# Attention and routed experts in one kernel: three routing groups, row clearing by AND, zero fills after the attention, a different pacing at the end, and two chunks of angles on GpSimd

## The chip, the cores and the metric

The kernel runs on one core of one Trainium2 chip. A core has a matrix engine (TensorE, PE in the profile; PEld is its weight load), VectorE (DVE), ScalarE (ACT), GpSimd (POOL) and SyncE (SP, which here only issues DMAs). Each engine works through its own list of instructions in order; semaphores tie the lists together, and 16 DMA engines move data. The metric is the device time of one launch in microseconds (us), as the median of several runs.

## The reference

Input is x of shape 16 x 512 x 128 (16 sequences of 512 tokens), all in float32. Two blocks follow each other.

```python
# block 1: causal linear attention, 16 heads of 8
q, k, v = split(silu(x @ Wq)), split(silu(x @ Wk)), split(x @ Wv)
q, k = lrpe(q, theta), lrpe(k, theta)     # concat(t * cos(theta * n), t * sin(theta * n)), n the position
energy = einsum('bhnd,bhmd->bhnm', q, k) * tril
out = merge(einsum('bhnm,bhmd->bhnd', energy, v)) @ Wo * sigmoid(x @ G1 @ G2)
x = layernorm(x + layernorm(out) * gamma + beta)
# block 2: 8 experts, each token goes to its two best, 1280 places per expert
probs = softmax(rmsnorm(x) @ router_w.T);  topk_p, topk_i = top_k(probs, 2)
# expert e takes the first 1280 of its tokens in order; places past its count weigh 0
eout = (silu(xg @ rg) * (xg @ ru)) @ rd
routed = zeros.at[dispatch].add(eout * weight)
shared = silu(x @ sg) * (x @ su) @ sd
x = layernorm(x + shared + routed)
```

There are T = 8192 tokens in 64 tiles of 128 (NT), four tiles or chunks to a sequence (NC).

## The kernel before

**The stages.** First come the loads and small constants, then the attention with the routing, then the experts, then the end, in which the routed rows are added and normed. The shared branch (`shared_steps`) is a filler of matmul work that runs beside the other stages. It is a list `feed` of 384 steps: for each sequence 16 "up" steps (gate at L134, up at L147; two for each of eight slices of 128) and 8 "down" steps (L157), the down steps of a sequence standing behind the first four up steps of the next. The order of PE, ScalarE, VectorE and GpSimd is written out by the program (`manual_schedule`).

**The opening.** The attention needs cosine and sine of theta times position for the four chunks of a sequence. `angles(c, th)` makes the reduced angle on VectorE, `sines(c)` the values on ScalarE, `same(c)` a copy of half of them. Chunks 0 and 1 are made ahead of the first step; chunks 2 and 3 at the loop's steps t=0 and t=1 (`beginning`). The causal mask and a block mask are made by GpSimd. Two tiles of constants are filled by ScalarE (`nought`): `zero` at t=0 and `empty` at t=1. From t=1 to t=16 `fill` issues one DMA a step on SP's queue: eight of 1 MB that zero `y_dram`, and eight of 660 KB that write `empty` (a row of zeros with the target number NOBODY) to `xg_dram`.

**The attention loop** runs t from -2 to 64, one chunk of 128 tokens a step. A step projects chunk t+2 (`project`: queries, keys, values and gate, then the multiply `hat`, L448), transposes chunk t+1 (`turn_over`), makes the energies of chunk t (L506 on PE, the masked copies `et` at L513 on VectorE), and the values of chunk t-1 (L530 to L548), and keeps a running state (`remember`; its addition L495 is on GpSimd). Up to two shared steps lie in a step once a sequence is ready, from t=14 on. When a sequence has ended, `after(b)` (turns over some ten steps) projects the output, norms twice and makes the router's logits. It has an addition on GpSimd, L564.

**Routing.** The list `groups` says which sequences are routed together: seven groups. `route(b0, b1)` is a generator of some 30 small VectorE instructions over [128, tiles, 8] with one Exp on ScalarE and two matmuls for the prefix sums. `sprinkle` puts up to seven of its steps into an attention step and three into a step behind it. A routed tile gives two scatters: indirect DMAs by GpSimd that send its 128 rows of 132 numbers (x, token number, expert, two weights) to places in `xg_dram` (L733). They go two a step in the attention, one in two steps behind it.

**Behind the attention** (called the tail here) a second loop goes on with one shared step each until turns, routes and scatters are done, and 12 steps more (`over`).

**The experts.** `load_expert` brings weights and 1280 rows; `turn_rows` transposes rows by PE (L899) and copies them (L900) in three parts of 512, 512 and 256 rows; `targets_of` takes target row and weight out of the extra columns (L907 to L913). For each part four slices of gate and up (L1008, L1010), the product (L1013), and `back`, which multiplies by rd (L922), weighs (L926) and scatters to `y_dram` (L928). The next expert's rows are turned in the slots `aside` of the part before, one slot a slice. A row whose target is out of bounds is not written.

**The end** runs what is left of `feed`. `add_up` adds the two routed rows of a sequence, on every other step; `finish_lot` takes a lot (four tiles of a sequence, or one tile in the last sequence) through statistics of each tile, the root, the scaled copies (L981) and the store. `an_end` calls the first of three open lots that can go on; it is called once a step, and the loop goes on when `feed` is empty.

Of the kernel before, what the change touches and what calls it, by code (L numbers as in the profile page):

```python
# [10 lines left out]
F32 = mybir.dt.float32  # L11
# [8 lines left out]
P = 128  # L20
# [8 lines left out]
NOBODY = 1.0e6  # L29
# [17 lines left out]
def tile_kernel(  # L47
# [46 lines left out]
    idx = keep.tile([P, 2, NT], I32, name="idx")  # L94
    sg_sb = keep.tile([P, IS], F32, name="sg_sb")
# [95 lines left out]
    groups = [(0, 4), (4, 8), (8, 10), (10, 12), (12, 14), (14, 15), (15, 16)]  # L191
    with ExitStack() as ph:
# [21 lines left out]
        with tc.manual_schedule(engines=ORDERED):  # L214
# [63 lines left out]
            def nought(tile_, n):  # L278
                nc.scalar.copy(tile_, zcol.to_broadcast([P, n]))
# [3 lines left out]
            th_sb = cst.tile([P, D + HALF], F32, name="th_sb")  # L283
# [14 lines left out]
            zero = hp.tile([P, 4 * N], F32, tag="h", name="zero")  # L298
            empty = hp.tile([P, NS, R], F32, tag="h", name="empty")
            scratch = hp.tile([P, 10, D + HALF], F32, tag="h", name="scratch")  # L300
            turns_of = cst.tile([P, D + HALF], F32, name="turns_of")
# [32 lines left out]
        with tc.manual_schedule(engines=ORDERED):  # L334
# [27 lines left out]
            count = cst.tile([P, E], F32, name="count")  # L362
# [4 lines left out]
            toki = cst.tile([P, NT], I32, name="toki")  # L367

        def constants_of_routing():
# [12 lines left out]
            nc.vector.tensor_copy(x1[:, :, D], toki)  # L382

        def beginning(t):

            if t == -1:
                sines(1)
            elif t == 0:
                angles(2, th_sb)
                sines(2)  # L390
            elif t == 1:
                angles(3, th_sb)
# [12 lines left out]


        y_rows = y_dram.rearrange("(p q r) d -> p q (r d)", p=P, r=4 * N // D)
        x_rows = xg_dram.rearrange("(p q r) d -> p q (r d)", p=P, r=NS)

        def fill(i):  # L410
            if i < 8:
                nc.sync.dma_start(y_rows[:, i, :], zero)
            elif i < 16:
                nc.sync.dma_start(x_rows[:, i - 8, :], empty.rearrange("p r d -> p (r d)"))

        hats, qkt, ets, states, gates, oTs = {}, {}, {}, {}, {}, {}
# [211 lines left out]
        def route(b0, b1):  # L628
# [75 lines left out]
            inside = wide("inside")  # L704
# [9 lines left out]
            rank = wide("rank")  # L714
# [83 lines left out]
        with tc.manual_schedule(engines=ORDERED):  # L798
            for t in range(-2, NT + 1):
# [14 lines left out]
                if 1 <= t < 17:  # L814
                    fill(t - 1)
# [31 lines left out]
            while turns or todo or scatters or over:  # L847
                if not (turns or todo or scatters):
                    over -= 1
# [11 lines left out]
                if t % 2 == 0:  # L861
                    scatter_behind(latest[0])
                t += 1


    with ExitStack() as ph:
# [23 lines left out]
        xgTs, targets = {}, {}  # L890
# [11 lines left out]
        def targets_of(e):  # L902
# [6 lines left out]
            nc.vector.scalar_tensor_tensor(to, second, float(T), xg[:, :, D], ALU.mult, ALU.add)  # L909
            wt = ep.tile([P, NS], F32, tag="wt", name=f"wt_{e}")  # L910
# [81 lines left out]
        with tc.manual_schedule(engines=ORDERED):  # L992
            load_expert(0)
            load_expert(1)
            for o0, n in parts:
                turn_rows(0, o0, n)
            targets_of(0)
            backs = []
            for e in range(E):
                rg_sb, ru_sb, rd_sb, _ = got[e]  # L1000
                for o0, n in parts:
                    aside = []
                    if o0 == parts[1][0] and e + 1 < E:
                        aside = [lambda q=q: turn_rows(e + 1, *q) for q in parts] + [lambda: targets_of(e + 1)]
# [29 lines left out]
            while feed or ends:  # L1034
# [16 lines left out]
                an_end()  # L1051

# [44 lines left out]
```

## Time and profile before

| | |
|---|---|
| median of three runs | 878.83 us (878.65 to 879.22) |
| the profiled execution | 876.59 us, its span 874.7 us |
| mean granted PE clock | 0.987 |
| PE busy | 826.3 us, 94% |
| VectorE busy | 554.1 us, 63% |
| ScalarE busy | 449.4 us, 51% |
| GpSimd busy | 334.2 us, 38% |
| L412, fill of `y_dram` | 8 DMAs of 1024 KB, 11.5 us to landing |
| L414, fill of `xg_dram` | 8 DMAs of 660 KB, 9.2 us to landing |
| L733, scatters to `xg_dram` | 128, 1039 ns each, from 181.6 to 494.6 us |
| L928, scatters to `y_dram` | 80, 972 ns each, from 516.8 to 726.5 us |

The span is cut into 40 slices of 21.9 us in some rows: each digit is the busy share of a slice in tenths, and PEclk the TensorE clock that was granted, in tenths of the full one. A line of the timeline has start and duration in us, engine, source line, operation, the tile written and those read, and the number of instructions merged; in brackets stands the idle time ahead of it and what ended it. A line of the waits has who waited and for whom, the sum in us, how often, and the longest.

### The profile page before, as it was taken

To read this page: it belongs to the slowest core of one execution; us is meant where nothing else is said; L and a number is where in the kernel's file an instruction comes from. 1 tells how busy PE (TensorE), PEld (TensorE's weight loads), DVE (VectorE), ACT (ScalarE), POOL (GpSimd) and SP (SyncE) were. 2 spreads that over 40 slices of the span, in tenths; PEclk is the share of its full clock that TensorE was granted. 3 is DMA by queue.
4 is the path that set the end of the run, shared out by engine and by line. 5 is a ranking of instruction groups with operands and counts; after the bars stand their busy time and mean duration, and the time that the engine had idled before them with its cause. 6 is when DMAs were issued, how large, how long until landed. Compare 5 with 4: busy or idle time off the path is not lost. (4 is left out here: it accounts for less than half of the span.)

```text
span 874.7 us, 24501 instructions
## 1 busy us (share of the span) xinstructions
PE 826.3 (94%) x9792; PEld 567.3 (65%) x9792; DVE 554.1 (63%) x1705; ACT 449.4 (51%) x1302; POOL 334.2 (38%) x443
## 2 busy tenths in 40 slices
PE   6789999999989999999999999999999999999993
PEld 4566667667855765766666657777676776666663
DVE  7588888998888888978533343333333324785454
ACT  7677777577776767564322223333333332433434
POOL 2122222156655556486766413433333431001100
PEclk9899999999999999999999999999999999999997
DMA  7881111011111110000000233322132003650011
GB/s 215 323 343 34 32 34 33 30 36 58 58 40 52 57 52 27 22 29 16 11 6 1 87 88 92 95 80 65 60 92 64 25 25 112 178 169 25 25 37 48
DMA packets 64340, 62.87 MB, mean 72 GB/s; under 512 B 6180, under 2 KB 55132, under 8 KB 63202
## 3 DMA queue, kind: packets, MB, share of 16 engines
q1 hardware_dynamic: 57426, 50.35, 18.4%
q0 software_dynamic: 6656, 10.69, 3.7%
q8 instruction: 77, 1.26, 0.6%
q10 hardware_dynamic: 144, 0.26, 0.1%
q14 instruction: 37, 0.30, 0.1%
HBM read 32.62 MB, written 31.88 MB: 74 GB/s over the span
## 5 line engine op out<-in xcount | busy, mean ns | idle before, releaser
L733 POOL DMA_INDIRECT xg_dram<-x,idx x128 | 133.0, 1039 | 42.1 <-issue 36.7
L136 ACT ACTIVATE sl<-pg 128x512 f32<-128x512 f32 x128 | 76.2, 596 | 125.4 <-PE pg L134 124.6
L1013 DVE TENSOR_TENSOR eh<-esl,peu 128x512 f32<-128x512 f32 (+1 forms) x96 | 57.5, 599 | 127.8 <-PE peu L1010 127.8
L928 POOL DMA_INDIRECT y_dram<-y,to x80 | 77.8, 972 | 154.1 <-ACT y L926 154.1
L148 DVE TENSOR_TENSOR h<-sl,pu 128x512 f32<-128x512 f32 x128 | 87.5, 684 | 77.0 <-PE pu L147 64.6
L134 PE MATMUL pg<-x1T,sg_sb 128*128 128x512 f32 x256 | 131.9, 597 | 1.5 <-ACT sl L136 0.7
L147 PE MATMUL pu<-x1T,su_sb 128*128 128x512 f32 x256 | 131.0, 593 | 1.0 <-ACT sl L136 1.0
L513 DVE TENSOR_TENSOR et<-pe,causal 128x384 f32<-128x384 f32 x256 | 124.4, 547 | 9.6 <-PE pe L506 9.5
L157 PEld LDWEIGHTS pd<-sd_sb,h 128*128 128x128 f32 x1024 | 118.7, 192 | 5.8 <-issue 5.2
L157 PE MATMUL pd<-sd_sb,h 128*128 128x128 f32 x1024 | 121.9, 275 | 0.2 <-DVE add L494 0.2
L110 POOL TENSOR_TENSOR rstd<-ve,neghalf 128x4 f32<-128x4 f32 x44 | 47.2, 1073 | 194.2 <-DVE ve L108 168.0
L922 PEld LDWEIGHTS ped<-rd,eh 128*128 128x128 f32 x640 | 84.0, 192 | 24.6 <-issue 22.7
L1008 PE MATMUL peg<-xgT,rg 128*128 128x512 f32 (+1 forms) x192 | 84.6, 522 | 0.0
L1010 PE MATMUL peu<-xgT,ru 128*128 128x512 f32 (+1 forms) x192 | 84.4, 521 | 0.0
L922 PE MATMUL ped<-rd,eh 128*128 128x128 f32 x640 | 84.3, 275 | 0.0
L1012 ACT ACTIVATE esl<-peg 128x512 f32<-128x512 f32 (+1 forms) x96 | 50.5, 526 | 55.9 <-PE peg L1008 53.9
L147 PEld LDWEIGHTS pu<-x1T,su_sb 128*128 128x128 f32 x256 | 45.7, 190 | 46.0 <-issue 39.9
L926 ACT ACTIVATE y<-ped,wt 128x128 f32<-128x128 f32 x80 | 29.4, 368 | 84.6 <-PE ped L922 84.6
L134 PEld LDWEIGHTS pg<-x1T,sg_sb 128*128 128x128 f32 x256 | 44.3, 191 | 38.4 <-issue 33.7
L506 PE MATMUL pe<-q,kT 32*64 32x192 f32 x2048 | 62.1, 341 | 3.3 <-issue 2.8
L423 PE MATMUL pq<-W,xT 128*128 128x384 f32 x128 | 60.3, 554 | 4.6 <-ACT vlow L444 2.6
L448 DVE TENSOR_TENSOR hat<-qk,cst_tok 128x512 f32<-128x512 f32 x64 | 45.0, 704 | 20.4 <-ACT qk L431 20.3
(178 smaller groups left out, 1260.4 us busy)
## 6 DMA issues: line engine op xcount, KB each, us to landing
y_dram<-zero SPq DMA_DIRECT2D x8, 1024.0 KB, 11.5
y<-y_dram SPq DMA_DIRECT2D x32, 256.0 KB, 3.3
xT<-xt SPq DMA_DIRECT2D x15, 384.0 KB, 3.1
xg_dram<-empty SPq DMA_DIRECT2D x8, 660.0 KB, 9.2
xg<-xg_dram SPq DMA_DIRECT2D x8, 660.0 KB, 4.5
x<-x SPq DMA_DIRECT2D x16, 256.0 KB, 3.5
o<-res SPq DMA_DIRECT2D x15, 256.0 KB, 2.3
xg_dram<-x,idx POOLq DMA_INDIRECT x128, 2.3
```

What stands on the lines that cost most here:

```text
L134: nc.tensor.matmul(pg, sg_sb[:, ts(i, P)], seq, start=True, stop=True)
L136: nc.scalar.activation(sl, pg, AF.Silu)
L147: nc.tensor.matmul(pu, su_sb[:, ts(i, P)], seq, start=True, stop=True)
L148: nc.vector.tensor_tensor(h[i // half][:, i % half, :], h.pop(("s", i)), pu, ALU.mult)
L157: nc.tensor.matmul(pd, h[k][:, i - k * half, ts(c, P)], sd_sb[:, i, :], start=(i == 0), stop=(i == IS // P - 1))
L506: nc.tensor.matmul(pes[g][mine, s], kT[rows, s, mine], q2[rows, s, 3 * i : 3 * i + 3], start=(s == 0), stop=(s == 1),)
L513: nc.vector.tensor_tensor(et.rearrange("p s k n -> p s (k n)"), pes[g].rearrange("p s k n -> p s (k n)"), causal.rearrange("p k n -> p (k ...
L733: i = nc.gpsimd.indirect_dma_start(out=xg_dram[:, :], out_offset=bass.IndirectOffsetOnAxis(ap=idx[:, k, t : t + 1], axis=0), in_=x1[:, t, ...
L922: nc.tensor.matmul(pd, h[:, i, ts(c, P)], got[e][2][:, i, :], start=(i == 0), stop=(i == IR // P - 1))
L928: i = nc.gpsimd.indirect_dma_start(out=y_dram[:, :], out_offset=bass.IndirectOffsetOnAxis(ap=to[:, at : at + 1], axis=0), in_=y, in_offset ...
L1008: nc.tensor.matmul(pg[:, :n], rg_sb[:, ts(i, P)], xgTs[e][:, ds(o0, n)], start=True, stop=True)
L1010: nc.tensor.matmul(pu[:, :n], ru_sb[:, ts(i, P)], xgTs[e][:, ds(o0, n)], start=True, stop=True)
```

## The change

The routing groups become three: sequences 0 to 5, 6 to 11 and 12 to 15. `inside` and `rank` use the buffers of `sel` and `prob`.

`empty` and its eight fills of `xg_dram` are dropped, so places that no token takes hold whatever memory held. `clear_rows` sets such rows to zero after the load by an AND with a mask made from the expert's `count`, and their targets are put out of bounds by an OR. It is called part by part ahead of `turn_rows`, for expert 0 ahead of all of them, for the others in the slots `aside`, which now run over from the second part into the third.

The fills of `y_dram` become 16 of 512 KB, read from 512 zero columns in the first `vpads` tile, and are issued in the tail, one in four steps. The tail goes on until they are issued.

In the end `an_end` is called a second time on every odd step, and on every step when `feed` is empty.

The angles of chunks 2 and 3 (the third and fourth) are made by GpSimd, right behind its masks, in nine instructions each; at t=0 and t=1 VectorE makes only the absolute value, now by an AND that clears the sign bit.

```diff
-    groups = [(0, 4), (4, 8), (8, 10), (10, 12), (12, 14), (14, 15), (15, 16)]
+    groups = [(0, 6), (6, 12), (12, 16)]
...
+        def sizes(c):
+            nc.vector.tensor_scalar(
+                scratch[:, NC + c].bitcast(I32), scratch[:, c].bitcast(I32), 0x7FFFFFFF, None, ALU.bitwise_and
+            )
+
         def angles(c, th):
-            a, size, k, whole = scratch[:, c], scratch[:, NC + c], scratch[:, 8], scratch[:, 9]
+            a, size, by = scratch[:, c], scratch[:, NC + c], scratch[:, 2 * NC]
             both = ((slice(0, D), pos[:, 0, c : c + 1]), (slice(D, D + HALF), pos[:, 1, c : c + 1]))
+            on_vector = c < 2
+            engine = nc.vector if on_vector else nc.gpsimd
             for m, at in both:
-                nc.vector.tensor_scalar(k[:, m], turns_of[:, m], at, MAGIC, ALU.mult, ALU.add)
-            nc.vector.tensor_scalar(whole, k, MAGIC, -C1, ALU.subtract, ALU.mult)
+                engine.tensor_scalar(size[:, m], turns_of[:, m], at, MAGIC, ALU.mult, ALU.add)
+            engine.tensor_scalar(a, size, MAGIC, -C1, ALU.subtract, ALU.mult)
             for m, at in both:
-                nc.vector.scalar_tensor_tensor(a[:, m], th[:, m], at, whole[:, m], ALU.mult, ALU.add)
-            nc.vector.tensor_scalar(k, k, MAGIC, -C2, ALU.subtract, ALU.mult)
-            nc.vector.tensor_tensor(a, a, k, ALU.add)
-            nc.vector.scalar_tensor_tensor(size, a, -1.0, a, ALU.mult, ALU.max)
-            nc.vector.tensor_scalar(a, a, -PI_BELOW, PI_BELOW, ALU.max, ALU.min)
+                if on_vector:
+                    engine.scalar_tensor_tensor(a[:, m], th[:, m], at, a[:, m], ALU.mult, ALU.add)
+                else:
+                    engine.tensor_scalar(by[:, m], th[:, m], at, None, ALU.mult)
+            if not on_vector:
+                engine.tensor_tensor(a, a, by, ALU.add)
+            engine.tensor_scalar(size, size, MAGIC, -C2, ALU.subtract, ALU.mult)
+            engine.tensor_tensor(a, a, size, ALU.add)
+            if on_vector:
+                sizes(c)
+            engine.tensor_scalar(a, a, -PI_BELOW, PI_BELOW, ALU.max, ALU.min)
...
+            for c in range(2, NC):
+                angles(c, th_sb)
...
         def beginning_done(t):
-            if t == 0:
-                nought(zero, 4 * N)
-            elif t == 1:
-                nought(empty.rearrange("p r d -> p (r d)"), NS * R)
-                nc.gpsimd.memset(empty[:, :, D], NOBODY)
-            elif t == 2:
+            if t == 2:
                 constants_of_routing()
...
-                if 1 <= t < 17:
-                    fill(t - 1)
...
+            zero = vpads[0][0].rearrange("p a b d -> p (a b d)")[:, 0:N]
+            nought(zero, N)
-            while turns or todo or scatters or over:
-                if not (turns or todo or scatters):
+            while turns or todo or scatters or fills or over:
+                if not (turns or todo or scatters or fills):
                     over -= 1
...
+                if t % 4 == 1 and fills:
+                    fill(fills.pop(0))
...
+        def clear_rows(e, o0, n):
+            if o0 == 0:
+                taken[e] = ok = ep.tile([P, 2, NS], I32, tag="ok", name=f"ok_{e}")
+                nc.vector.tensor_scalar(ok[:, 0], slotno, count[:, e : e + 1], -1.0, ALU.is_lt, ALU.mult)
+                nc.vector.tensor_scalar(ok[:, 1], slotno, count[:, e : e + 1], float(NOBODY), ALU.is_ge, ALU.mult)
+            here = slice(o0 // P, (o0 + n) // P)
+            rows = got[e][3][:, here, :].bitcast(I32)
+            nc.vector.tensor_tensor(
+                rows, rows, taken[e][:, 0, here].unsqueeze(2).to_broadcast([P, n // P, R]), ALU.bitwise_and
+            )
...
+            nc.vector.tensor_tensor(to, to, taken[e][:, 1], ALU.bitwise_or)
...
+            for o0, n in parts:
+                clear_rows(0, o0, n)
             for o0, n in parts:
                 turn_rows(0, o0, n)
...
-                        aside = [lambda q=q: turn_rows(e + 1, *q) for q in parts] + [lambda: targets_of(e + 1)]
+                        for step in (clear_rows, turn_rows):
+                            aside += [lambda q=q, f=step, e=e: f(e + 1, *q) for q in parts]
+                        aside.append(lambda e=e: targets_of(e + 1))
...
                 an_end()
+                if begun % 2 == 1 or not feed:
+                    an_end()
```

More of the change, by code (lines that the diff above doesn't have):

```diff
@@ L28 @@
 R = D + 4
-NOBODY = 1.0e6
+NOBODY = 1 << 20
 LN_EPS = 1e-5
@@ L94, in tile_kernel @@
     idx = keep.tile([P, 2, NT], I32, name="idx")
+    count = keep.tile([P, E], F32, name="count")
+    slotno = keep.tile([P, NS], F32, name="slotno")
     sg_sb = keep.tile([P, IS], F32, name="sg_sb")
@@ L282, in tile_kernel @@
             nc.tensor.matmul(pth, ones[0:1, :], th_row, start=True, stop=True)
-            th_sb = cst.tile([P, D + HALF], F32, name="th_sb")
+            th_sb = wk1.tile([P, D + HALF], F32, tag="w", name="th_sb")
             nc.scalar.copy(th_sb, pth)
@@ L297, in tile_kernel @@
             cst_tok = cst.tile([P, NC, 2, 16, 2, 8], F32, name="cst_tok")
[L298 to L301, printed above, removed]
+            scratch = hp.tile([P, 2 * NC + 1, D + HALF], F32, tag="h", name="scratch")
+            turns_of = wk1.tile([P, D + HALF], F32, tag="o", name="turns_of")
@@ L361, in tile_kernel @@
             startrow = cst.tile([P, E], F32, name="startrow")
-            count = cst.tile([P, E], F32, name="count")
             goes_on = {}
@@ L367, in tile_kernel @@
             toki = cst.tile([P, NT], I32, name="toki")
+            sloti = cst.tile([P, NS], I32, name="sloti")
         def constants_of_routing():
@@ L382, in constants_of_routing @@
             nc.vector.tensor_copy(x1[:, :, D], toki)
+            nc.gpsimd.iota(sloti, pattern=[[P, NS]], base=0, channel_multiplier=1)
+            nc.vector.tensor_copy(slotno, sloti)
         def beginning(t):
@@ L388, in beginning @@
             elif t == 0:
-                angles(2, th_sb)
+                sizes(2)
                 sines(2)
             elif t == 1:
-                angles(3, th_sb)
+                sizes(3)
                 sines(3)
         def beginning_done(t):
-            if t == 0:
-                nought(zero, 4 * N)
-            elif t == 1:
-                nought(empty.rearrange("p r d -> p (r d)"), NS * R)
-                nc.gpsimd.memset(empty[:, :, D], NOBODY)
-            elif t == 2:
+            if t == 2:
                 constants_of_routing()
-        y_rows = y_dram.rearrange("(p q r) d -> p q (r d)", p=P, r=4 * N // D)
-        x_rows = xg_dram.rearrange("(p q r) d -> p q (r d)", p=P, r=NS)
+        y_rows = y_dram.rearrange("(p q r s) d -> q p r (s d)", p=P, r=2, s=N // D)
         def fill(i):
[L411 to L414, printed above, removed]
+            nc.sync.dma_start(y_rows[i], zero.unsqueeze(1).to_broadcast([P, 2, N]))
+        fills = list(range(2 * T * D // (P * 2 * N)))
         hats, qkt, ets, states, gates, oTs = {}, {}, {}, {}, {}, {}
@@ L703, in route @@
             nc.scalar.copy(tots[:, :, 1:], pin[:, 1].rearrange("p t e -> p e t"))
-            inside = wide("inside")
+            inside = rp.tile([P, n, E], F32, tag="sel", name=f"inside_{b0}")
             nc.scalar.copy(inside, pin[:, 0])
@@ L713, in route @@
             yield
-            rank = wide("rank")
+            rank = rp.tile([P, n, E], F32, tag="prob", name=f"rank_{b0}")
             nc.vector.tensor_tensor(rank, sums[:, :, :n].rearrange("p e t -> p t e"), inside, ALU.add)
@@ L888, in load_expert @@
             got[e] = rg_sb, ru_sb, rd_sb, xg
-        xgTs, targets = {}, {}
+        xgTs, targets, taken = {}, {}, {}
+        def clear_rows(e, o0, n):
[8 more added lines that the diff above has]
+            )
         def turn_rows(e, o0, n):
@@ L995, in tile_kernel @@
             for o0, n in parts:
+                clear_rows(0, o0, n)
+            for o0, n in parts:
                 turn_rows(0, o0, n)
             targets_of(0)
-            backs = []
+            backs, aside = [], []
             for e in range(E):
@@ L1001, in tile_kernel @@
                 for o0, n in parts:
-                    aside = []
                     if o0 == parts[1][0] and e + 1 < E:
-                        aside = [lambda q=q: turn_rows(e + 1, *q) for q in parts] + [lambda: targets_of(e + 1)]
+                        for step in (clear_rows, turn_rows):
+                            aside += [lambda q=q, f=step, e=e: f(e + 1, *q) for q in parts]
+                        aside.append(lambda e=e: targets_of(e + 1))
                     h = ep.tile([P, IR // P, N], F32, tag="eh", name=f"eh_{e}_{o0}")
```

## The prediction

> **What bounds the kernel now.** I read the page's slices first, then TensorE's waits in the opening, then the starts of the 64 hat multiplies (L448, one per attention step), and last the stretch behind the last matmul.
>
> ```profile
> PE   6789999999989999999999999999999999999993
> PEclk9899999999999999999999999999999999999997
> DMA  7881111011111110000000233322132003650011
> GB/s 215 323 343 34 32 34 33 30 36 58 58 40 52 57 52 27 22 29 16 11 6 1 87 88 92 95 80 65 60 92 64 25 25 112 178 169 25 25 37 48
> ...
> q8 instruction: 77, 1.26, 0.6%
> ```
>
> TensorE (PE) sets the time: busy 826.3 of 874.7 us. The 48.4 us of idle lie at both ends: 16.3 us before 60 us (windows 0:20, 20:40, 40:60), where the DMA engines are full, and 13.9 us behind the last shared matmul. Between them, a busy PE can still be a slow one, so there I go by step lengths.
>
> ```profile
> PE pout L548 <- issue: 3.1, 1, 3.1
> PE pq L423 <- ACT vlow L444: 2.6, 1, 2.6
> ...
> PE pe L506 <- issue: 2.2, 1, 2.2
> ...
> PE pout L539 <- issue: 1.4, 1, 1.4
> ```
>
> Three of PE's long waits before 60 us wait for no engine ("issue"), and all fall while the zero fills run (issued 20.2 to 57 us, 8 x 1024 KB and 8 x 660 KB, landing after 11.5 and 9.2 us where a 256 KB load takes 3.5). The instruction queue's packets are 16 KB each, and the last packets before two of the stalls ended at 30.8 and 38.0 us, some 1.3 us before PE went on (32.2, 39.3): PE ran out of instructions. After the gaps at 20.6 and 36.2 us the granted clock is half for 3.4 us.
>
> **Fills moved (13.5 MB out of the opening, 8.4 MB into the tail).** The hats of steps without an `after` turn are 2.97 us apart (26.7 to 29.7). The next two gaps are 5.07 and 8.03 us, with the stalls in them: three steps to 42.8 us take 16.1 us and would take 8.9, so **7.1 us**. The next four take 19.6 us and the four after the fills 19.1: **0.5 us**. The rule that speaks against this is the Trainium skill's "Runtime: NRT & Kernel Launch", section Instruction fetch mechanics: an engine fetches its next 16 KiB block ahead, and crossing a boundary is mostly hidden. By the rule alone these 7.6 us would not come back; the rows show fetches late only under the fills, so I take the rows. ScalarE's copy into `zero` (1.90 us at 18.3) hides behind the angles; the one into `empty` (1.30 us at 25.0) holds the next qk activation, whose matmul ended at 25.2, until 26.2: **1.0 us**. In the tail, PE fetches a block each 23 to 27 us and a fill comes alone every fourth step (3.5 us), 512 KB at the 368 GB/s of window 20:40, so 1.4 us of DMA: cost 0, up to 4.7 if stalls go with the bytes (7.6 x 8.4/13.5). SP's queue has only these fills there until the experts' loads; 16 of them take 64 steps, inside the tail's length. The one 512-column copy on ScalarE is hidden (busy 39.7 of 119 us from 385 to 504).
>
> **Angles of chunks 2 and 3 on GpSimd.** DVE now makes them at 12.3 to 14.8 and 18.7 to 21.4 us (2.6 us each), and sines follow at 14.56 and 21.16. GpSimd is free from 9.4 us (its last causal select). Each chunk is nine instructions there. No row has this tensor_scalar on GpSimd; nearest are affine_select 128x128 0.28 us, tensor_tensor 128x128 0.46 (L495) and 128x512 1.27 (L564), so 192 columns of two inputs cost 0.6. By the first, one chunk is 3.8 us, by the second 5.0; I take 4.4. Undisturbed: done at 13.8 and 18.2, DVE's new AND (0.26) at once, sines near 14.1 and 19.1: 2.5 us won. But the port speaks against it:
>
> ```profile
> 245.21 1.16 POOL L604 TENSOR_TENSOR rms<-sq,neghalf 128x4 f32<-128x4 f32 x1
> ...
> 245.97 1.79 DVE L661 TENSOR_TENSOR prob<-prob,tot 128x128 f32<-128x128 f32 x1
> 246.35 1.26 POOL L564 TENSOR_TENSOR x<-x,bet 128x512 f32<-128x512 f32 x1
> ```
>
> L661 takes 0.29 us alone and here 1.79: it ends 0.15 us behind GpSimd's second instruction. The hat at 175.9, met by L564, takes 1.54 us for 0.69. The Trainium skill's "SBUF — State Buffer", section Who interferes with whom, says that a DVE instruction with two SBUF inputs and a GpSimd one that reads SBUF lock each other out for one instruction. By the rule the hats at 10.1 and 11.2 us lose up to 0.6 us each; by the row a waiting DVE can sit through several if GpSimd leaves no gap. Its dependent instructions do leave 0.07 us (L346 to L347). I take 0.4 us for each hat and 0.1 for each copy (`same`), 1.0 us in all, and GpSimd held back 1.5 us by them: sines of chunk 2 at 15.6 (1.0 late), of chunk 3 at 20.5. Net **0.6 us** won; ends +2.5 and -6 (no gap at all: first hat at 18.2 rather than 10.1, with 2 won back). Behind the AND on DVE stand only its own chunk's copy and hat, and at t=1 the et multiplies; behind chunk 3 on GpSimd stands the state add (18.95), which is wanted a step later. The first `after` finds the work buffers that now hold th_sb and turns_of long free. Opening: 7.1 + 0.5 + 1.0 + 0.6 = **9.2 us**.
>
> **Three routing groups for seven.** A group is 31 DVE instructions (8.8 us at 16 tiles, 6.9 at 8 without the locked L661) and two activation table loads of 1.28 us on ScalarE, whatever its size. Steps with scatters and no routing are 5.67 us apart (hats 33 to 40), with neither 5.63 (17 to 24). The eight or seven steps of the first four groups take 4.5, 6.6, 4.0 and 6.2 us more, 21.3 in all. Following the loops step by step, the attention keeps two groups, of 24 tiles each: 10.7 us of DVE by the slope of 0.24 us a tile, so 5.3 + 1.1 = 6.4 us each. 21.3 - 12.9 = **8.4 us**, between 4 (price goes with elements) and 10.6 (goes with groups). In the tail, 383.8 to 429.6 us holds 10.3 us more than its shared steps at 0.86 and 0.89; some 6.7 is matmul work of the last turns and routes; one group of three stays there, at t=88 to 101: **2.0 us** (0 to 3.5). The buffers now shared (`inside` in `sel`, `rank` in `prob`) add no wait: the matmuls that free `sel` make `inside`, and `prob` was read long before.
>
> Scatters begin later (t=37 for 29): 40 wait at the tail's start for 24, and the tail grows from 124 to 156 steps. These are shared steps that PE has to do anyway; 126 for 158 are left for the end. Cost 0: both places run at 0.86 a step.
>
> **Clearing rows.** `empty` goes; per expert three ANDs of 528, 528 and 264 columns (0.71, 0.71, 0.37 by the hat row) and three small ones at 0.17 come to DVE, 2.3 us. DVE is busy 17 of 50 us there, and PE waits at none of the seven later transposes (its waits 500:730 show e=0 alone), so they hide; uncovered they would cost 16 us. The next expert's transposes move three slots back, into the 256-row part, all ahead of its first matmul. For expert 0 all three stand ahead of the copies:
>
> ```profile
> 504.71 1.07 PE L899 MATMUL ept<-ident,xg 128*128 128x128 f32 x8 [0.93 <-issue]
> 505.44 1.65 DVE L900 COPY xgT<-ept 128x512 f32<-128x512 f32 x3 [0.82 <-PE ept L899]
> ...
> 506.46 1.02 PE L1008 MATMUL peg<-xgT,rg 128*128 128x512 f32 x2
> ```
>
> DVE is free at 504.6, so ANDs end at 506.3, and the first expert matmul follows the first copy by 1.0: 507.4. **Cost 1.0 us** (0.5 to 3).
>
> **Denser end.**
>
> ```profile
> 860.84 0.29 DVE L162 TENSOR_TENSOR x1T<-pd,x 128x128 f32<-128x128 f32 x1 [1.49 <-PE pd L157]
> ...
> 863.50 1.65 ACT L981 ACTIVATE res<-x1T,nb,rstd 128x128 f32<-128x128 f32 x4 [0.44 <-DVE nb L978]
> ...
> 871.65 0.49 ACT L981 ACTIVATE res<-x1T,nb,rstd 128x128 f32<-128x128 f32 x1 [0.47 <-ACT root L116]
> ```
>
> Behind the last shared step two full lots and four single ones remain; counting the loop's calls gives the same six. With three calls per two steps, and 126 steps, it leaves four single lots, the first with its statistics made. A single lot takes 1.15 us (867.45 to 868.60). So the last result starts at 861.4 + 3 x 1.15 = 864.9 for 871.65: **6.7 us** (5 to 7.5). Had only the steps shrunk, nine lots would remain. The load fits: with 0.60 us for a product, 0.61 for an addition and 0.40 for a tile's statistics (from start to start) the count gives DVE 76.6 us of work in 110 us of end steps, and never over 1.6 us behind.
>
> **Sum.** 9.2 + 8.4 + 2.0 - 1.0 + 6.7 = 25.3 us. The profiled execution (span 874.7, 876.6 with what lies around it) would come to 851.3; the median shown is 2.2 above that execution, so **853.5 us**.
>
> **Rivals.** (1) GpSimd leaves no gap and the first hats wait for both chunks: 6 lost for 0.6 won, 860.1. For it: L661. Against: the 0.07 us gaps. (2) Routing costs DVE time by elements elsewhere and nothing of the 10.4 comes: 863.9. Against: groups of half the size cost as much. (3) The fills stall PE in the tail as they do now: 858.2. (4) The slower one: GpSimd's two-operation tensor_scalar is as costly as its pow, which takes 1.04 us for 4 columns (L110). Chunk 3's sines come at 21.2 now; to eat the other 24.7 us its angles must end at 46 us, 36.5 us for 18 instructions. From **2.03 us each** the kernel is slower; at 2.2 it is 882. Against: every plain GpSimd row here is 0.2 to 1.3 us. That the end isn't denser: 853.5 with 9 lots would be 870; the loop's text excludes it.
>
> **Chances.** Forecast 0.65, (1) 0.15, (2) 0.10, (3) 0.06, (4) 0.04. Range 846 (start 12, routing 14, end 7.5) to 865, which takes in (1) to (3). A measurement tells 0.2% (1.8 us) from none: faster 0.94, same 0.02, slower 0.04.
>
> **What will show it.** Hat 7 near 34 us rather than 42.8, no "issue" wait over 1 us before 60, no half clock near 39. Hats 0 and 1 under 1.2 us long; over 3 is rival 1. Two routes before the tail, at 6 to 7 us of longer steps each. L1008 about 3 us behind the xg landing. Four single lots behind the last L157. A PE wait for "issue" in the tail would make the fills' zero wrong.

## The result, and the profile after

The changed kernel takes 870.82 us (median of 4, 867.75 to 871.79) against 878.95 us for the kernel before, run beside it on the same chip: a ratio of 0.9902, 95% interval 0.9877 to 0.9926. It is 8.1 us faster, a third of the 25.3 us that the prediction adds up to, and 5.8 us above the top of its range. The profiled execution took 870.6 us, its span 868.9.

First the page of the changed kernel: the rows by slices (40 of 21.7 us), and the new fills among the DMA issues.

```profile
PE   5999999988999998899999998999999999999896
...
PEclk9899999999999999999999999999999999999999
DMA  6011111110111110048000033221232110365211
GB/s 198 21 34 33 33 33 33 34 32 15 45 52 52 58 55 24 21 142 312 23 10 5 1 89 84 93 84 45 80 93 92 53 37 22 91 176 168 82 37 49
...
y_dram<-vpad SPq DMA_DIRECT2D x16, 512.0 KB, 7.1
```

The DMA row is nearly empty where the fills were (slices 2 and 3: 21 and 34 GB/s for 323 and 343) and PE is at 9 there for 7 and 8; the fills' new place is slices 18 and 19, where PE stays at 9. A new 8 stands near the end of PE's row, in slice 38 (803 to 825 us), where before there were only nines.

To find where the expected time went, I cut both profiled executions at events that both have, and set each stretch beside the prediction's term for it. A hat is the multiply of one attention step on VectorE, counted from 0. Shared steps of the tail ran at 0.86 and 0.89 us in both (0.87 on average), so the 32 steps that moved from the end to the tail count 27.8 us in each place.

| stretch | before, us | after, us | change without the 27.8 | predicted |
|---|---|---|---|---|
| start to hat 25 | 138.1 | 135.1 | -3.0 | -9.2 |
| hat 25 to hat 63 | 234.2 | 231.1 | -3.1 | -8.4 |
| hat 63 to the tail's last shared step | 130.5 | 154.2 | -4.1 | -2.0 |
| from there to the first expert product | 3.7 | 5.5 | +1.8 | +1.0 |
| experts, to the end's first shared step | 214.8 | 216.0 | +1.2 | 0 |
| end, to the last down step | 138.5 | 118.9 | +8.2 | 0 |
| behind it (the drain) | 14.9 | 8.2 | -6.7 | -6.7 |

The drain is what was predicted. The largest miss is the line above it: the end's own steps became slower. The waits of PE, then of VectorE, from 742 to 855 us in the changed kernel (sum in us, how often, the longest):

```profile
PE pd L159 <- DVE x1T L164: 5.7, 3, 2.9
```

```profile
DVE x1T L164 <- PE pd L159: 11.7, 9, 2.8
DVE nb L1001 <- POOL rstd L112: 9.2, 9, 1.2
...
DVE h L150 <- ACT sl L138: 8.1, 10, 1.0
```

PE, which before did not wait here, now waits for VectorE's copy out of a down step (L164), and VectorE sits 9.2 us at `nb`, the instruction of a lot that needs GpSimd's power. The timeline of the changed kernel shows how one becomes the other:

```profile
768.76 0.67 DVE L150 TENSOR_TENSOR h<-sl,pu 128x512 f32<-128x512 f32 x1
769.34 0.68 DVE L978 TENSOR_TENSOR x1T<-x1T,y 128x512 f32<-128x512 f32 x1
769.94 0.16 DVE L110 TENSOR_SCALAR ve<-mv 128x4 f32<-128x4 f32 x1
770.18 1.01 POOL L112 TENSOR_TENSOR rstd<-ve,neghalf 128x4 f32<-128x4 f32 x1 [6.71 <-DVE ve L110]
771.23 0.16 DVE L1001 SCALAR_TENSOR_TENSOR nb<-mv,rstd 128x4 f32<-128x4 f32 x1 [1.12 <-POOL rstd L112]
771.30 0.28 DVE L164 TENSOR_TENSOR x1T<-pd,x 128x128 f32<-128x128 f32 x1
771.42 1.65 ACT L1004 ACTIVATE res<-x1T,nb,rstd 128x128 f32<-128x128 f32 x4 [4.63 <-DVE nb L1001]
771.50 0.68 DVE L978 TENSOR_TENSOR x1T<-x1T,y 128x512 f32<-128x512 f32 x1
...
771.64 3.84 PE L159 MATMUL pd<-sd_sb,h 128*128 128x128 f32 x32 [1.68 <-DVE x1T L164]
```

VectorE has nothing between `ve` and `nb`: it waits 1.12 us for a power on four columns. Behind `nb` in its list stands the copy of a down step, and PE, which wants that PSUM buffer back, waits 1.68 us. In `finish_lot` one call that does nothing stands between the root and `nb`. At one call a step it spread the two over a step of other work; when a second call follows at once, it spreads them over nothing.

### The profile page after: what moved, and what is told of

The parts are those of the page before. It is cut to its first block, busy times and chain, and to the rows that moved or that the text cites. A ratio compares the mean times of both kernels' runs of the same rounds, so it can differ in the third digit from the quotient of the medians.

```text
span 868.9 us, 24377 instructions
## 1 busy us (share of the span) xinstructions
PE 827.3 (95%) x9776; PEld 568.8 (65%) x9776; DVE 550.0 (63%) x1613; ACT 433.2 (50%) x1279; POOL 349.7 (40%) x469
## 5 line engine op out<-in xcount | busy, mean ns | idle before, releaser
L951 POOL DMA_INDIRECT y_dram<-y,to x80 | 77.6, 970 | 156.8 <-ACT y L949 156.8
L150 DVE TENSOR_TENSOR h<-sl,pu 128x512 f32<-128x512 f32 x128 | 87.6, 684 | 75.1 <-PE pu L149 55.5
L520 DVE TENSOR_TENSOR et<-pe,causal 128x384 f32<-128x384 f32 x256 | 124.4, 547 | 10.9 <-PE pe L513 10.6
L159 PE MATMUL pd<-sd_sb,h 128*128 128x128 f32 x1024 | 124.4, 278 | 5.9 <-DVE x1T L164 5.7
L112 POOL TENSOR_TENSOR rstd<-ve,neghalf 128x4 f32<-128x4 f32 x46 | 50.1, 1088 | 195.4 <-DVE ve L110 188.9
L159 PEld LDWEIGHTS pd<-sd_sb,h 128*128 128x128 f32 x1024 | 120.6, 194 | 12.1 <-DVE x1T L164 6.3
L513 PE MATMUL pe<-q,kT 32*64 32x192 f32 x2048 | 63.5, 344 | 0.8 <-DVE et L520 0.8
L1036 PEld LDWEIGHTS peu<-xgT,ru 128*128 128x128 f32 x192 | 36.8, 192 | 32.8 <-issue 29.5
```

The source lines that it names most:

```text
L150: nc.vector.tensor_tensor(h[i // half][:, i % half, :], h.pop(("s", i)), pu, ALU.mult)
L159: nc.tensor.matmul(pd, h[k][:, i - k * half, ts(c, P)], sd_sb[:, i, :], start=(i == 0), stop=(i == IS // P - 1))
L513: nc.tensor.matmul(pes[g][mine, s], kT[rows, s, mine], q2[rows, s, 3 * i : 3 * i + 3], start=(s == 0), stop=(s == 1),)
L520: nc.vector.tensor_tensor(et.rearrange("p s k n -> p s (k n)"), pes[g].rearrange("p s k n -> p s (k n)"), causal.rearrange("p k n -> p (k ...
L951: i = nc.gpsimd.indirect_dma_start(out=y_dram[:, :], out_offset=bass.IndirectOffsetOnAxis(ap=to[:, at : at + 1], axis=0), in_=y, in_offset ...
L1036: nc.tensor.matmul(pu[:, :n], ru_sb[:, ts(i, P)], xgTs[e][:, ds(o0, n)], start=True, stop=True)
```

## The experiments

Three sets of kernels ran on different chips, each beside the kernel before, whose medians were 884.86, 877.16 and 877.84 us; ratios are therefore compared, and stretches within a set where that is possible. In the first set (the undone end, all angles on VectorE, seven groups, 8.4 MB of fills in the opening) even like stretches are longer: hat 63 to the tail's last shared step takes 157.4 to 157.7 us with three groups, and 153.9 to 154.2 in the other sets with as many steps. The totals in this set's expectations were worked out for the chip of the first measurement; a ratio times 878.95 us is set against them. In the second set the changed kernel ran once more, as a yardstick.

> The changed kernel itself, to stand beside the others of this call on one chip. Both theories: the ratio to the kernel before is within 0.9877 and 0.9926, the end stage holds some 8 us of stalls, 9 waits of VectorE for GpSimd's pow.

It took 871.55 us, ratio 0.9926 (0.9904 to 0.9947), span 870.3; its stretches are within 0.5 us of the first time, except the start to hat 25: 136.6 for 135.1 us.

### The denser end

**Undone alone.**

```diff
                 an_end()
-                if begun % 2 == 1 or not feed:
-                    an_end()
```

> The changed kernel (870.8 us) with an_end called once a step, as before the change. Theory: the denser calls themselves make VectorE late in the end stage (it sits behind GpSimd's pow, some 1 us for each of nine lots) and cost 10 us of TensorE stalls, so the stalls of 742 to 861 us go (under 2 us left), but nine lots stay behind the last matmul and need about 20 us: 872 to 874. Rival: the stalls come from having 126 end steps rather than 158 for the same additions and loads, whatever the calls: they stay, and the drain is added, 880 to 884.

881.64 us, ratio 0.9964 (0.9949 to 0.9979), which is 875.8 us on the first chip, between the two expected totals. The stalls are gone, as the theory had it. The drain is 21.6 us for 8.2: without the second call nine lots are left, as the prediction's count had it. The end's stretch falls to 110.7 us. Busy times from the first end steps to 822 us (stretch, its length, PE, weight loads, VectorE and so on, granted clock), here and in the changed kernel:

```profile
746.00:822.00 76.00, 76.00 (x382) 50.65 (x381) 51.25 (x139) 25.79 (x53) 9.59 (x10) 1.00 0.47 136
```

```profile
742.00:822.00 80.00, 74.30 (x362) 49.80 (x361) 54.66 (x162) 28.73 (x63) 12.48 (x12) 0.98 0.47 135
```

PE is busy all 76.00 us without the second call and idle 5.7 of 80 with it; the half clock that follows a pause, 3.4 us at 818.4, adds some 1.7. So the denser end brings 13.4 us in the drain and loses 8.1 in front of it. VectorE is busy 67% and 68% in the two: it is not full. At one call a step its waits of `nb` for the power are 1.4 us in sum, for 9.2.

**The wait taken out of the denser end.** The same instructions, but a lot whose power is under way lets the next lots be called instead:

```diff
             if not roots:
-                yield True
+                yield False
+                yield False
```

> The changed kernel, in which a lot that has just issued its pow gives its next two calls to the following lots, so that VectorE comes to nb two end steps later. Theory (the wait for the pow): VectorE's 9 waits of about 1 us go and with them most of the 8.1 us of TensorE stalls in the end; under 2.5 us of stalls stay, 5 to 6.5 us faster than the changed kernel of this call. Rival (sheer load: additions, products and statistics on VectorE and scaled copies ahead of silu on ScalarE): the waits go but 5 us and more of stalls stay, at most 3 us faster.

860.61 us, ratio 0.9813 (0.9781 to 0.9845), 10.9 us below the yardstick. The wait of `nb` for the power is no longer among VectorE's, and of PE's there is left, from 742 to 855 us:

```profile
PE pd L159 <- DVE x1T L164: 1.7, 3, 0.8
```

The timeline of this kernel around the same lot:

```profile
767.74 0.17 DVE L110 TENSOR_SCALAR ve<-mv 128x4 f32<-128x4 f32 x1
...
767.98 1.01 POOL L112 TENSOR_TENSOR rstd<-ve,neghalf 128x4 f32<-128x4 f32 x1 [6.32 <-DVE ve L110]
...
768.80 0.68 DVE L978 TENSOR_TENSOR x1T<-x1T,y 128x512 f32<-128x512 f32 x1
...
769.40 0.15 DVE L1002 SCALAR_TENSOR_TENSOR nb<-mv,rstd 128x4 f32<-128x4 f32 x1
```

`nb` stands behind six other VectorE instructions and finds the power ready. The end's stretch is 113.3 us for the yardstick's 118.9 (5.6 less), and as the calls that did nothing now do work, two lots fewer are left: drain 5.9 for 8.2. These 7.9 us are the edit's. VectorE's waits for ScalarE's `sl`, 8.1 us as changed, are still 6.3 here, so by themselves they stall PE little. The other 3.2 us of the shorter span come ahead of the end, where this edit changes nothing: 2.0 by hat 25, with a half clock of 6.8 us for 10.2 in the opening, and 1.2 by hat 63.

### The opening

**All four angles on VectorE**, the rest as changed (`on_vector = True`, both calls back at t=0 and t=1).

> The changed kernel with all four chunks of angles on VectorE again. Theory: GpSimd's chains of 6.5 us each hold the sines of chunks 2 and 3 back by 2.1 and 2.3 us, and the longer TensorE pauses bring 10 us at half clock; on VectorE the hats 2 to 4 come 2 to 3 us earlier and the kernel takes 867 to 868.5. Rival: the opening is bound by ScalarE and the projections anyway, with a pause of nearly the same length: 870 to 871.5.

874.05 us, ratio 0.9869 (0.9843 to 0.9894), which is 867.4 us on the first chip, as the theory had it. The ratio is below both measurements of the changed kernel, 0.9902 and 0.9926; its interval overlaps the first one's and ends just below the second's. Hat 25 is at 132.5 us for 135.1 and 136.6: GpSimd's angles cost time. Their path in the changed kernel (timeline; only the lines that make up the chain):

```profile
13.86 0.87 POOL L325 TENSOR_SCALAR scratch<-scratch 128x192 f32<-128x192 f32 x1
...
14.81 0.59 POOL L326 TENSOR_TENSOR scratch<-scratch 128x192 f32<-128x192 f32 x1
...
15.49 0.86 POOL L329 TENSOR_SCALAR scratch<-scratch 128x192 f32<-128x192 f32 x1
...
16.39 0.26 DVE L305 TENSOR_SCALAR scratch<-scratch 128x192 int32<-128x192 int32 x1 [4.03 <-POOL scratch L329]
16.68 0.64 ACT L335 ACTIVATE cst_tok<-scratch,half_pi 128x128 f32<-128x128 f32 x2 [3.00 <-DVE scratch L305]
...
17.57 0.25 ACT L437 ACTIVATE qk<-pq 128x128 f32<-128x128 f32 x1
...
18.02 0.69 DVE L455 TENSOR_TENSOR hat<-qk,cst_tok 128x512 f32<-128x512 f32 x1 [0.24 <-ACT qk L438]
...
18.86 0.63 PE L468 MATMUL pt<-ident,hat 128*128 128x128 f32 x4 [3.06 <-DVE wo_sb L816]
```

The addition of 192 columns takes 0.59 us, as estimated; the tensor_scalars with two constants of the same width take 0.86 to 0.89. Where a hat met this work, it was GpSimd that waited: a multiply of 128 columns took 1.12 us beside the hat at 18.02, for 0.61 elsewhere. A chunk takes 6.5 us (9.89 to 16.35, then to 22.9). The sines start at 16.68 and 23.47, 2.1 and 2.3 us later than before, and PE pauses 3.06 us, behind which the clock is half for 10.2 us (19.6 to 29.8).

**Only the fourth chunk on GpSimd**, the third back on VectorE at t=0:

```diff
-            on_vector = c < 2
+            on_vector = c < 3
...
-            for c in range(2, NC):
-                angles(c, th_sb)
+            angles(3, th_sb)
```

> The changed kernel with the third chunk's angles on VectorE at step 0, as before, and only the fourth chunk's on GpSimd. Theory (length of the GpSimd chain): one chain of 6.5 us ends at about 16.4 us, ahead of the 18.8 at which VectorE asks for it; sines of both chunks come earlier than in any kernel so far (14.6 and 19.1 us), TensorE's pause near 20 falls under 1.5 us; hat 7 at 34.5 to 36, 3 to 4.5 us faster than the changed kernel. Rival (the shared port): VectorE's multiplies with two inputs in SBUF are what GpSimd's work delays, hats 0 and 1 above 1 us long, less than 1.5 us won.

864.11 us, ratio 0.9841 (0.982 to 0.9863), 7.4 us below the yardstick. Hat 7 starts at 35.5 us for the yardstick's 40.4 and the changed kernel's 39.7, and the clock is at half nowhere before 60 us. GpSimd has the fourth chunk ready at 15.5, 4.6 us before it is wanted. One chunk there pays, two do not: the second is what comes late.

**The fills back in the opening.** First only the bytes that the changed kernel fills: the sixteen 512 KB fills at t=1 to 16, none in the tail.

```diff
+            if t == 0:
+                nought(zero, N)
...
+                if 1 <= t < 17:
+                    fill(fills.pop(0))
```

> The changed kernel with its 16 fills of 512 KB back in steps 1 to 16 (the fills of the row buffer stay away). Theory: the zero fills starve TensorE's instruction fetch in the opening and cost nothing in the tail: waits for issue of 1 us and more come back between 25 and 60 us, 3 to 6 us in all, 874 to 876.5. Rival: the fills cost as much in the tail as in the opening, or the opening is bound by the angles and the half clock anyway: 869.5 to 871.5.

876.84 us, ratio 0.9917 (0.9895 to 0.9938), no different from the changed kernel: 871.6 us on the first chip, the rival's number. But PE waits for instructions 2.3 us in two places, and the steps from hat 6 to hat 8 take 10.6 us for 7.9; but the step from hat 16 to hat 17, which a half clock makes 8.05 us long in the changed kernel, takes 6.53 here, and hat 25 is at 135.1 in both. The waits that came back and the half clocks that stayed away (3.4 us for 10.2 before 60 us, and none at hat 16) cancel by chance.

```profile
PE pout L558 <- issue: 2.3, 2, 1.7
```

This kernel also shows what the fills cost in the tail: without them, hat 63 to the tail's last shared step takes 157.7 us, and with them, in the undone end of the same set, 157.7. In the changed kernel's tail PE has no wait for "issue" over 0.3 us.

Then all 13.5 MB, with ScalarE's copies and with all angles on VectorE, to be set against the kernel with the angles on VectorE:

> The changed kernel with all four chunks' angles on VectorE, and with all the old fills (eight of 1 MB, eight of 0.66 MB, and ScalarE's copies for them) back in the first seventeen steps; the AND stays. Set against the kernel with all angles on VectorE and the fills behind the attention, whose 25th hat starts at 132.5 us and whose ratio is 0.9869. The forecast's terms: 8.6 us later at the 25th hat (7.1 of steps, 0.5 and 1.0 of the rest), PE waiting for its instructions by some 6 us. Theory now: 4 to 6 us later, since a step that is free of fills takes 3.6 us and not the 2.97 the forecast took; ratio 0.992 to 0.994.

873.09 us, ratio 0.9943 (0.9923 to 0.9962). Hat 25 is at 139.3 us for 132.5, 6.8 us later: between the two expectations, nearer to the new one. PE's waits from 0 to 60 us have the "issue" ones back:

```profile
PE pout L563 <- issue: 2.8, 1, 2.8
...
PE pe L521 <- issue: 1.1, 1, 1.1
```

Each of these two, and a third of 1.1 us at 63.5, ends 1.3 to 1.5 us behind the end of a 16 KB packet of the instruction queue (37.8, 56.0 and 62.1 us), as before the change and as with the 8.4 MB (36.7 us, PE on at 38.2).

### The routing groups

**Seven groups again**, the rest as changed.

> The changed kernel with the seven routing groups of before. Theory: routing costs by VectorE time and a bit by group: the attention's four groups take 21 us of longer steps for 18 with two large ones, the tail some 2 to 4 us more; the end has 158 steps again and is less crowded (2 to 6 us less stall) and one to two lots fewer wait behind it: within 867 to 874. Rival by elements alone: attention and tail as now, the end better: 863 to 866. Rival by groups alone (my forecast's term): attention 8 us longer, 876 to 880.

878.92 us, ratio 0.9932 (0.9913 to 0.9952), which is 873.0 us on the first chip, in the theory's range. Against the undone end of the same set, which has three groups, hats 25 to 63 take 236.5 us for 232.3 (4.2), and hat 63 to the last shared step of the tail 136.0 us for 157.7, of which 27.8 are the 32 steps (6.1). But 1.85 us of that are part of the expert start: PE waits for a product `h` that stands on VectorE behind the first expert's ANDs. Here this falls ahead of the last shared product, in the undone end behind it:

```profile
506.76 1.12 PE L149 MATMUL pu<-x1T,su_sb 128*128 128x512 f32 x2 [1.85 <-DVE h L150]
```

The pause behind that product is 4.4 us, for 5.9 in the undone end. So three groups bring 8.5 us (4.2 and 4.3), for 10.4 predicted, and the total ratio differs far less. With seven groups 32 more shared steps lie in the end, and the lots have more steps to hide in: the drain is 5.9 us for 8.2, and the end takes 6.5 us more than before for the same 158 steps, where the changed kernel loses 8.2 in 126.

**At most four routing instructions in a step**, in place of seven (`sprinkle(t, 3)` and `sprinkle(t, 4)` become 2 and 2).

> The changed kernel with at most four routing instructions in an attention step instead of seven. Theory (an attention step has some 1.5 us of VectorE to spare, and seven instructions of 0.36 us overflow it): hats 25 to 63 take 4 to 8 us less than in the changed kernel of this call (231 us there). Since scatters start later, the tail has 12 to 24 more steps and the end fewer, which may give part of it back. Rival (each us of routing costs the same wherever it stands): hats 25 to 63 within 2 us of the changed kernel.

868.82 us, ratio 0.9893 (0.9862 to 0.9923). Hats 25 to 63 take 227.1 us for the yardstick's 231.0, as the theory said, but not for its reason. The first group lies whole between hats 33 and 43 in both, and gains next to nothing: 63.3 us for 63.9, each with a half clock near 194 us (62.5 in four kernels with seven a step whose half clock comes some 16 us further on). The gain lies behind hat 57, since 11 of the 61 routing instructions, 4.4 us of VectorE, have moved behind hat 63; and beyond its 12 more steps the tail is 3.4 us longer. So the rival's reading holds: routing costs about the same wherever it stands. In the end, now 12 steps shorter, 5.5 us of stalls and half clock go, and the drain is 4.5 us longer (12.7 for 8.2). Of the 2.9 us by which the span is shorter, 2.2 come ahead of hat 25, where this edit changes nothing.

### The expert start

**The first expert's ANDs between the transposes**: each part is cleared and then turned, together with the two edits of the combined kernel below.

```diff
-            for o0, n in parts:
-                clear_rows(0, o0, n)
             for o0, n in parts:
+                clear_rows(0, o0, n)
                 turn_rows(0, o0, n)
```

> As the first kernel of these, with the ANDs over the first expert's rows made part by part, each just ahead of that part's transposes, instead of all of them ahead of the first transpose. Theory: the pause of PE between the last shared product of the tail and the first expert product (5.3 us in the changed kernel, 3.7 before it) is the row of ANDs, so it falls to about 4 us, and the half-clock stretch of 3.4 us at the first expert may go with it: 1 to 4 us less than the first kernel. Rival: the wait is for the load of the rows as a whole, and the pause stays within 0.3 us: same time.

860.1 us, ratio 0.9794 (0.9778 to 0.981), slower than the combined kernel. Both expectations fall: the pause became 7.2 us, and the half clock 6.8 us long. The timelines say why, first the changed kernel's:

```profile
520.35 1.02 PE L149 MATMUL pu<-x1T,su_sb 128*128 128x512 f32 x2
...
520.97 1.33 DVE L910 TENSOR_TENSOR xg<-xg,ok 128x528 int32<-128x528 int32 x2 [2.24 <-DMA xg<-xg_dram]
522.22 0.68 DVE L150 TENSOR_TENSOR h<-sl,pu 128x512 f32<-128x512 f32 x1
522.81 0.42 DVE L910 TENSOR_TENSOR xg<-xg,ok 128x264 int32<-128x264 int32 x1
523.16 0.68 DVE L150 TENSOR_TENSOR h<-sl,pu 128x512 f32<-128x512 f32 x1
...
523.94 1.12 PE L921 MATMUL ept<-ident,xg 128*128 128x128 f32 x8 [2.57 <-DVE h L150]
...
525.83 1.92 PE L1034 MATMUL peg<-xgT,rg 128*128 128x512 f32 x2
```

and that of the kernel with the ANDs between:

```profile
517.59 0.97 PE L920 MATMUL ept<-ident,xg 128*128 128x128 f32 x4 [1.40 <-DVE xg L909]
518.60 0.69 DVE L921 COPY xgT<-ept 128x512 f32<-128x512 f32 x1 [1.06 <-PE ept L920]
519.20 0.42 DVE L909 TENSOR_TENSOR xg<-xg,ok 128x264 int32<-128x264 int32 x1
...
519.77 0.66 PE L920 MATMUL ept<-ident,xg 128*128 128x128 f32 x2 [1.21 <-DVE xg L909]
...
520.23 1.06 PE L1033 MATMUL peg<-xgT,rg 128*128 128x512 f32 x1
```

As changed, VectorE waits 2.24 us for the rows with the last two shared products (L150) behind that wait in its list, then works through the ANDs and the products, and only the last product lets the transposes begin. Before, those products were done at 504.62, and the transposes began at 504.71. With the ANDs between, each copy stands ahead of the next AND in VectorE's list, so PE and VectorE take turns: transposes, copy, AND, transposes. An order that puts the two products ahead of the first AND was not tried. The later experts' ANDs are hidden, as predicted: where no half clock falls at the start, in the combined kernel, the experts' stretch is 214.8 us, as before.

### Edits put together

**The skipped power wait and the fourth chunk alone on GpSimd.**

> The changed kernel with two edits at once: the tail's normalisation skips two calls while GpSimd has the power (instead of asking for one more), and only the fourth chunk's angles stay on GpSimd. Theory: the two act in different places (opening, end of the shared output's additions), so their gains add: about 10.9 us and 7.4 us measured singly against a twin of the changed kernel, of which some 2 us was luck of the opening, so 16 to 18 us: a ratio of 0.971 to 0.976 to the kernel before. Rival: the gains overlap, because both singles had an opening without a half-clock stretch by chance: then about 12 us, ratio 0.979 to 0.982.

856.5 us (855.89 to 858.78), ratio 0.9761 (0.9743 to 0.9779): better than the changed kernel by 1.4 to 1.65 percentage points. Span 854.3 us, 16.0 below the yardstick's: hat 25 is 5.6 us earlier, the end's stretch is 5.3 us shorter, the drain 2.3, hats 25 to 63 1.5, and the experts, which here have no half clock at their start, 1.3. The gains add, at the edge of what was expected.

**The same with thin routes, and two calls in every end step** (with three skipped calls behind the power).

> As the previous kernel, with at most four routing instructions in a step of the attention instead of seven, and two calls of the end queue in every step with three skipped ones behind the power. Theory: the attention gains the 3.9 us it gained when thinned alone, the tail loses 12 more steps of shared products only in place (the work is the same), the end keeps no more than two lots behind the last product, so 3 to 5 us less than the previous kernel, ratio 0.967 to 0.972. Rival: twice the calls in every step overfill VectorE, PE waits in the shared steps behind the experts by more than 5 us in sum, and the time is no better than the previous kernel's.

864.06 us, ratio 0.9837 (0.9816 to 0.9859), worse than without these two: the rival holds. Hats 25 to 63 gain 2.4 us, and the tail gives 3.4 back. In the end, from 744 to 858 us, PE waits again for the copy of a down step,

```profile
PE pd L159 <- DVE x1T L164: 7.0, 3, 3.9
```

and this time not behind the power: VectorE's wait for it is 0.8 us in sum. VectorE is busy only 77.7 of 114 us, so again it is the order and not the sum; that more of the lots' work now stands ahead of the shared copies is the likely reading. Ahead of the longest wait, VectorE also stood 1.0 us for ScalarE's `sl`, which came behind a scaled copy. No further run tested either, nor were the two edits tried apart.

## Why the prediction was wrong, step by step

Its first reading, that PE's 48.4 us of idle lie at both ends, leaves out 18.2 us between 60 and 861 us, most of them from 150 to 400; since it went by step lengths there, no term hangs on it.

**"The load fits" (denser end): wrong, the costliest step.** The prediction said that the count "gives DVE 76.6 us of work in 110 us of end steps, and never over 1.6 us behind", and took no cost. The work was right (77.6 us busy from 740 to 862), but the count left out a wait inside the list: some 1 us at each lot for GpSimd's power, with PE's PSUM copies behind it. The prediction had the power's 1.04 us in hand, and used it only for the angles. It cost 8.2 us. The undone end shows that the second call brings the stall, the skipped calls that the order around the power makes most of it. The gain of the drain, 6.7 us, came as worked out, with four single lots 1.15 us apart; ScalarE's line in the changed kernel:

```profile
862.38 0.49 ACT L1004 ACTIVATE res<-x1T,nb,rstd 128x128 f32<-128x128 f32 x1 [1.34 <-DVE nb L1001]
...
863.56 0.49 ACT L1004 ACTIVATE res<-x1T,nb,rstd 128x128 f32<-128x128 f32 x1 [0.47 <-DVE nb L1001]
...
864.71 0.49 ACT L1004 ACTIVATE res<-x1T,nb,rstd 128x128 f32<-128x128 f32 x1 [0.47 <-ACT root L118]
...
865.87 0.49 ACT L1004 ACTIVATE res<-x1T,nb,rstd 128x128 f32<-128x128 f32 x1 [0.47 <-ACT root L118]
```

**Routing groups: the group's price in the attention too low, part handed back.** 10.4 us were predicted; 7.2 came before against after, 3.1 in the attention for 8.4 and 4.1 in the tail for 2.0 (4.2 and 4.3 against seven groups). The step that failed is the 6.4 us for a group of 24 tiles: the two made their steps 8.3 us longer (6.8 in executions whose half clock falls elsewhere) and 9.3. The 10.7 us of VectorE for such a group were near the mark (23.0 us for the two); what failed is the step that only half of them would lengthen the steps. VectorE was busy 45.1 of 50 us from 250 to 300 before, so little room was left, and thinning showed that the work costs and not its density. That the tail gained twice what was priced made up for a part, by luck. The term "cost 0" for the steps that move to the tail held for those steps themselves. It missed that a shorter end has fewer steps to hide lots in: with seven groups two lots fewer were left behind, 2.3 us.

**Fills: mechanism right, up to 1.8 us too large.** The issue waits are gone, come back with the bytes (2.8 and 1.1 us), and the fills cost nothing in the tail. The rows, not the Trainium skill's rule on block fetches ("Runtime: NRT & Kernel Launch", Instruction fetch mechanics), told what happens under full DMA. The mis-sized term is the free step of 2.97 us: it was a step that caught up, and steps free of fills take 3.59. The three steps gained 4.4 us for 7.1; the four behind them 1.5 for 0.5. The measured sum, with 0.9 for the copy into `empty`, is 6.8 for 8.6. Of the 1.8 us missing, 0.9 are rather the angles': the first of the three steps took 4.49 us at the half clock behind their pause, and takes 3.60 where only the fourth chunk is on GpSimd and no half clock comes.

**Angles: wrong sign.** 0.6 us won was predicted, and the two steps that wait for chunks 2 and 3 lost 2.3. "I take 4.4" for a chunk, between affine_select and tensor_tensor, was the step that failed: the tensor_scalar with two constants is slower than either, and the chunk 6.5. The Trainium skill's "GPSIMD Engine Reference", section Engine selection, puts one-input work at about line rate and two-input work at half the speed; here one input with two constants on 192 columns takes 0.86 to 0.89 us against 0.26 on VectorE, two inputs 0.59 against 0.36, so for one input the measurement decides against it. The first rival did not occur: hats 0 and 1 took 0.69 and 0.78 us. The slower rival's mechanism, a dear tensor_scalar, is what happened, but at 0.87 us and not at its 2.03, and not with every two-operation one: multiply and add took 0.36 us on 128 columns.

**Expert start: 1.0 predicted, 3.0 measured.** The prediction let the ANDs start when VectorE is free of the shared products; they stand ahead of the last two. That makes the pause 1.8 us longer, and the half clock behind it, which the prediction did not look for, makes the experts' stretch 1.2 us longer.

**Half clock at hat 16.** 1.5 us more in a step that the change does not touch: the clock was at half for 3.4 us at 81.1, behind a pause of 1.4 us. The same pause stood at 84.0 us before, and the clock stayed whole: bad luck, and no step of the prediction.

Added up: 8.2 (end) + 1.8 (fills) + 2.9 (angles) + 1.5 (hat 16) + 3.2 (routing, attention and tail together) + 2.0 (experts) = 19.6 us, which is what parts the predicted 25.3 from the 5.7 that the stretches give. The range missed because its cases varied what the prediction had priced; none priced a stall in the end.

## What to carry to other kernels

When a list is called more densely, do not only count the engine's load: walk each chain that leaves the engine and comes back, and ask what else now stands between the two ends. A wait on another engine, even 1 us for four columns, is paid by all that is queued behind it. And before a step length is taken as free, look whether its neighbours were late: a step that catches up is shorter than any that will be had.

## What was not expected of the hardware

- GpSimd's tensor_scalar goes neither by the number of inputs nor by that of operations. With two constants it took 0.86 to 0.89 us on 192 columns, where the two-input addition took 0.59. With one number per partition, multiply and add took 0.36 us on 128 columns, and the multiply alone 0.61.
- The clock came down for 3.4 us or multiples of it (6.8, 10.2). Behind the opening this followed pauses of PE of 1.4 to 3.9 us, but not each of them: the changed kernel's code has a pause of 1.42 us at 60.3 us in one execution and at 61.0 in the other, and a half clock behind it only in the second. Its hat 7 stood at 39.7 us once and at 40.4 once. Differences of 1 to 2 us between single executions are no evidence for or against an edit.
- With the fourth chunk alone on GpSimd, VectorE's pair of L320 took 1.04 us beside GpSimd's additions, for some 0.5 us of work undisturbed, as the port rule weighed in the prediction has it; that kernel still gained.
